# Third layer of a four-layer graph network: the accumulator banks are emptied by ScalarE copies and joined in SBUF; the fourth layer's score banks move

## Chip, cores and metric

One kernel runs on one core of a Trainium2 chip. The metric is device time in microseconds for one execution, the median of several runs. Matrix products, accumulated in PSUM, are TensorE's (PE in the profile). VectorE (DVE), ScalarE (ACT) and GpSimd (POOL) do the element-wise work, and SyncE (SP) issues most of the DMAs.

## The reference

Four layers of graph attention work one after another on the same 4096 nodes with 256 features, all with one 4096 x 4096 adjacency matrix, in float32. Each layer's result is added to its input and normalised. The change touches the third layer (`L2` in the reference) and the start of the fourth (`L3`):

```python
def _L2_gnn_ref(x, adj, W, a):
    h = x @ W
    e_src = h @ a[:D, 0]
    e_dst = h @ a[D:, 0]
    e = e_src[:, None] + e_dst[None, :]
    e = jnp.where(e > 0, e, NEG_SLOPE * e)
    att_logits = jnp.where(adj > 0, e, MASK_VAL)
    attention = jax.nn.softmax(att_logits, axis=1)
    h_prime = attention @ h
    return jax.nn.elu(h_prime)

def _L3_gnn_ref(features, adj, Wq, Wk):
    Qn = _cos_normalize(features @ Wq.T)
    Kn = _cos_normalize(features @ Wk.T)
    raw_att = Kn @ Qn.T
    att = jnp.where(adj > 0, raw_att, NEG) * TEMP
    att = jax.nn.softmax(att, axis=1)
    prop_fea = att @ features
    ...
    return (1.0 - KEEP_RATIO) * prop_fea + KEEP_RATIO * features

x = _layernorm(x + _L2_gnn_ref(x, adj, L2_gnn_W, L2_gnn_a), axis=-1)
x = _layernorm(x + _L3_gnn_ref(x, adj, L3_gnn_Wq, L3_gnn_Wk), axis=-1)
```

## The kernel before, in words

**Tiling.** The nodes are 32 tiles of 128. Output rows are taken in `NB` = 8 blocks of 512 (`QW`), and for every block the kernel walks over all 32 tiles of neighbours, two tiles at a time: `NP` = 16 units `g` for each block `b`.

**A unit of the third layer** (`additive_one`). The function `weights(b, g)` makes the unnormalised attention weights. For each of the two tiles ScalarE writes a factor `r` into one of two PSUM banks (L564), and VectorE turns it into `prob` with the mask (L565). From block 1 on, `mix_weights` forms four half-width sums and differences of `prob` for a seven-product scheme: one VectorE instruction (L434, both inputs in SBUF) and two GpSimd instructions (L435, L436). `sums(b, g)` then issues the matrix products (L444): seven products a unit from block 1 on, into four accumulator banks `acc0` to `acc3`; block 0 uses ordinary products (L579) into `acc0` and `acc1`. The first product of a unit writes `acc3`, the next two `acc0`, then two `acc1` and two `acc2`.

**Order.** The loop runs over units with a lag: iteration `i` makes the weights of unit `i` and the sums of unit `i - 3`. The order of TensorE, VectorE and ScalarE in this loop is the written one (`tc.manual_schedule`); GpSimd and the DMA queues are ordered by the framework's planner. The four accumulator banks have one copy, so the products of a new block write the banks that the block before has just filled, and these have to be read out in between. `prob` and `mix` have four buffers each.

**End of a block.** The iteration that sums unit 15 of block `b` comes to `weights(b + 1, 2)`. Before these weights are issued, `first_half` and `second_half` combine the four banks into the tile `quarters`: one ScalarE copy `one` (L449) and five VectorE additions that read one operand from PSUM (L450, L452, L453, L457, L458). In block 0 one ScalarE copy (L587) and two VectorE copies (L588, L589) do it.

**After a block.** While the next block runs, `finish` projects the four row tiles of the finished one (`project`, L594, products into the two `g` banks), takes them out of the bank (`take`: a VectorE reciprocal L600, ScalarE `e` L602 and `h` L603), adds and normalises them (L611, L612, L154, L155). From block 2 on, `follow.prepare` also prepares the fourth layer's inputs from the normalised rows: transposes by DMA (L127, L131, L135), products into both `g` banks (L1059, in the iteration of `g` = 8), squares, a root and scaling on ScalarE.

**Start of the fourth layer** (`cosine_attention`). Its code is outside the written order, so the planner places it. Scores (L1115) go to the two banks of the pool `co_pz`, and in later blocks also to `g`; ScalarE takes the exponential (L1119), VectorE masks (L1127) and mixes, and the same seven products follow. [...] The third layer's pools are opened in the order `gb_pr` (two factor banks), `gb_pa` (four accumulators), `gb_ps` (two `g` banks). The fourth layer's are opened as `co_pa`, `co_pz`, `co_ps`, so that its accumulators lie over the factor banks and `acc0`, `acc1`, and its score banks lie over `acc2`, `acc3` of the third layer.

Of the kernel before, what the change touches and what calls it, by code (L numbers as in the profile page):

```python
# [9 lines left out]
FP = mybir.dt.float32  # L10
# [4 lines left out]
OP = mybir.AluOpType  # L15
AX = mybir.AxisListType
PSUM = bass.MemoryType.PSUM

P = 128
# [3 lines left out]
QW = QB * P  # L23
# [5 lines left out]
def kernel(  # L29
# [27 lines left out]
    nc = tc.nc  # L57
    N = x.shape[0]
    NT = N // P
    NB = N // QW  # L60

    def pool(stack, name, bufs, **kw):
        return stack.enter_context(tc.tile_pool(name=name, bufs=bufs, reuse_waits="tile", **kw))
# [4 lines left out]
    fin1 = ctx.enter_context(tc.tile_pool(name="fin1", bufs=1))  # L68
# [352 lines left out]
    NP = NT // 2  # L421
    HW = QW // 2
# [9 lines left out]
    def mix_weights(s, z, eng):  # L432

        nc.vector.tensor_tensor(s[:, :2, :], z[:, 0, :].rearrange("p (h i) -> p h i", h=2), z[:, :, HW:], OP.subtract)  # L434
        eng.tensor_tensor(s[:, 2, :], z[:, 0, :HW], s[:, 1, :], OP.subtract)  # L435
        eng.tensor_tensor(s[:, 3, :], z[:, 1, :HW], s[:, 2, :], OP.subtract)  # L436

    def product(acc, z, s, t, g, n):

        even, odd = X[:, 2 * g, :D], X[:, 2 * g + 1, :D]  # L440
        at, half, w, a = ((3, 0, even[:, :P], z[:, 0, :HW]), (0, 0, odd[:, :P], z[:, 1, :HW]),
                          (0, 1, t[:, 1], s[:, 2]), (1, 0, t[:, 0], s[:, 1]), (1, 1, odd[:, P:], s[:, 3]),
                          (2, 0, t[:, 2], s[:, 0]), (2, 1, t[:, 3], z[:, 1, HW:]))[n]
        nc.tensor.matmul(acc[at][:, half * HW:(half + 1) * HW], w, a, start=(g == 0 and half == 0),  # L444
                         stop=(g == NP - 1), skip_group_check=True)

    def first_half(c, one, acc):

        nc.scalar.copy(one, acc[3][:, :HW])  # L449
        nc.vector.tensor_tensor(c[:, :2, :], one.unsqueeze(1).to_broadcast([P, 2, HW]),  # L450
                                acc[0].rearrange("p (h i) -> p h i", h=2), OP.add)
        nc.vector.tensor_tensor(c[:, 2, :], c[:, 1, :], acc[1][:, :HW], OP.add)  # L452
        nc.vector.tensor_tensor(c[:, 3, :], c[:, 2, :], acc[1][:, HW:], OP.add)  # L453

    def second_half(c, acc):

        nc.vector.tensor_tensor(c[:, 1:3, :], c[:, 1:3, :], acc[2][:, :HW].unsqueeze(1).to_broadcast([P, 2, HW]), OP.add)  # L457
        nc.vector.tensor_tensor(c[:, 1, :], c[:, 1, :], acc[2][:, HW:], OP.add)  # L458

    def quarters(c, k):  # L460

        lo = k % 2 * P
        return [c[:, q, lo:lo + P] for q in ((0, 3), (1, 2))[k // 2]]
# [61 lines left out]
    def additive_one(w_sb, ga, tail, op, follow):  # L525

        with ExitStack() as lay:
# [4 lines left out]
            sb = pool(lay, "gb_sb", 2)  # L532
# [9 lines left out]
            mixed, acc, prob, mix, mvs, roots, kept, drawn, ys, far_y = {}, {}, {}, {}, {}, {}, {}, {}, {}, {}  # L542

            def bank():
                return ps.tile([P, QW], FP, name="g")

            def weights(b, g):
                if b == 0 and g < 2:
                    mask = ga.first_mask[:, 2 * g:2 * g + 2, :]
                else:  # L550
                    mask = mp.tile([P, 2, QW], I32, name="mask")
                    nc.sync.dma_start(mask, edges[:, 2 * g:2 * g + 2, b * QW:(b + 1) * QW])
                if b < NB - 1:
                    if 4 <= g < 4 + QB:
                        ga.dots((b + 1) * QB + g - 4, (0,), sb, "h")
                    elif g == 8:
                        ga.sources(b + 1)
                    elif g == 11:
                        ga.row(b + 1, nc.sync)
                z = prob[b, g] = zp.tile([P, 2, QW], FP, name="prob")  # L560
                for n in range(2):
                    j = 2 * g + n
                    r = pr.tile([P, QW], FP, name="r")
                    nc.scalar.activation(r, ga.row_of(b), AF.Relu, bias=ga.less[:, j:j + 1], scale=ga.dst[:, j:j + 1])  # L564
                    nc.vector.scalar_tensor_tensor(z[:, n, :], r, ga.own[:, j:j + 1], mask[:, n, :], OP.add, OP.mult)  # L565
                if b:
                    s = mix[b, g] = zp.tile([P, 4, HW], FP, name="mix")
                    mix_weights(s, z, nc.gpsimd)

            def sums(b, g):  # L570
                if g == 0:
                    acc[b] = [pa.tile([P, QW], FP, name=f"acc{n}") for n in range(4)]
                if b:
                    for n in range(7):
                        product(acc[b], prob[b, g], mix[b, g], mixed[g // 2][:, g % 2], g, n)
                else:
                    for j in range(2 * g, 2 * g + 2):
                        for c in range(KC):
                            nc.tensor.matmul(acc[b][c], X[:, j, c * P:(c + 1) * P], prob[b, g][:, j % 2, :],  # L579
                                             start=(j == 0), stop=(j == NT - 1))  # L580
                if g == NP - 1:
                    c = kept[b] = op.tile([P, 4, HW], FP, name="quarters")
                    if b:
                        first_half(c, op.tile([P, HW], FP, name="one"), acc[b])
                        second_half(c, acc[b])
                    else:
                        nc.scalar.copy(c[:, :2, :], acc[b][0].rearrange("p (h i) -> p h i", h=2))  # L587
                        nc.vector.tensor_copy(c[:, 3, :], acc[b][1][:, :HW])  # L588
                        nc.vector.tensor_copy(c[:, 2, :], acc[b][1][:, HW:])  # L589

            def project(bank, b, k):
                po = drawn[b, k] = bank()
                for c, quarter in enumerate(quarters(kept[b], k)):
                    nc.tensor.matmul(po[:, :D + 1], quarter, w_sb[:, c, :D + 1], start=(c == 0), stop=(c == KC - 1))  # L594
# [52 lines left out]
            with tc.manual_schedule(engines=fixed):  # L647
                for i in range(len(units) + LAG):
                    b, g = units[i - LAG] if i >= LAG else (-1, 0)
                    if g == NP - 1:  # L650
                        sums(b, g)
                    if i < len(units):
                        weights(*units[i])
                    if b >= 0:
                        if g < NP - 1:
                            sums(b, g)
                        if b:
                            finish(b - 1, g)
                        else:
                            for _ in range(3 if g > 3 else 0):  # L660
                                next(before, None)
                            if g == 11:
                                follow.start()
                            elif g == 14:
                                follow.centre(bank())
                            if g % 2:
                                t = mixed[g // 2] = keep.tile([P, 2, 4, P], FP, name=f"mixed{g // 2}")
                                mix_features(t, g // 2)
                        if b > 1 and g in (2, 4, 6, 8, 9, 10, 11, 12, 13, 14, 15):
                            follow.prepare(bank, b - 2, 1, ys[b - 2])  # L670
                        if b == NB - 1 and g > 3 and g % 2 == 0:
                            q = g // 2 - 2
                            nc.scalar.dma_start(X[:, q * QB:(q + 1) * QB, :D], far_y[q])
                        if b == NB - 1 and g in (3, 5, 7):
                            follow.load_mask(0, (g - 3) // 2, prob[b, g][:, 0, :1])
# [411 lines left out]
    def cosine_attention(co, tail):  # L1087
# [4 lines left out]
        with ExitStack() as lay:  # L1092
            keep = pool(lay, "co_mixed", 1)
            sb = pool(lay, "co_sb", LAST + 1)
# [2 lines left out]
            co.turning = (pool(lay, "co_turn", 1), None,  # L1097
                          pool(lay, "co_turn_far", 2, space=bass.MemoryType.DRAM))

            pa = pool(lay, "co_pa", 1, space=PSUM)  # L1100
            pz = pool(lay, "co_pz", 2, space=PSUM)
            ps = pool(lay, "co_ps", 2, space=PSUM)
            ov = out.rearrange("(t p) d -> p t d", p=P)
            mixed, acc, prob, mix, y = {}, {}, {}, {}, {}
# [125 lines left out]
            for i in range(len(units) + LAG):  # L1230
                if i < len(units):
                    b, j = units[i]
# [5 lines left out]
                    if (b, j) in steps:  # L1238
                        n, step = steps[b, j]
                        co.prepare(bank, n, step, X[:, n * QB:(n + 1) * QB, :])  # L1240
                if i >= LAG:
                    b, j = units[i - LAG]
# [38 lines left out]
    with ExitStack() as weights1, ExitStack() as den1, ExitStack() as weights3:  # L1281
# [25 lines left out]
        op = weights3.enter_context(tc.tile_pool(name="gb_o", bufs=1))  # L1307
# [37 lines left out]
```

## Time and profile before

| what | value |
|---|---|
| median of 3 runs | 2818.91 us (2817.45 to 2821.47) |
| the profiled execution's own time | 2817.77 us |
| its span, first to last instruction | 2816.0 us |
| busy over the span: PE, DVE, ACT, POOL | 2784.7, 2274.4, 1695.6, 1050.6 us |
| third layer, blocks 1 to 7 (1772 to 2172 us): PE, DVE, ACT, POOL busy | 389.3, 329.9, 229.3, 197.7 of 400 us |
| passage to the fourth layer (2172 to 2186 us): PE, DVE, ACT, POOL busy | 10.9, 8.8, 5.0, 2.3 of 14 us |
| fourth layer (2186 to 2816 us): PE, DVE, ACT, POOL busy | 620.3, 429.8, 175.3, 46.6 of 630 us |
| mean granted TensorE clock over the span | 0.997 of full speed |

An engine is busy while it executes an instruction; register, branch, semaphore and DMA-issuing instructions are not counted. The profile pairs each idle stretch of an engine with the instruction or the DMA whose semaphore ended it. In a timeline a line has the start in microseconds from the first instruction, the duration of the merged group, the engine, the line of code, the operation, tiles written and read, the shape and the count. In brackets stands the idle time just before it and what ended it. One float32 product of this kernel shows as two matrix-product records and two weight loads.

### The profile page before, as it was taken

What the parts mean: (1) busy time and instruction counts of PE and PEld (TensorE: products, weight loads), DVE (VectorE), ACT (ScalarE), POOL (GpSimd) and SP (SyncE); (2) the same over time, 40 slices, a digit from 0 to 9 for tenths busy, and PEclk for the clock granted to TensorE, in tenths of its full rate; (3) what the DMA queues carried; (4) which work ended last, traced back from release to release, by engine and by line L of the source; (5) the groups of instructions that cost most, each with busy time, mean ns of one, the idle gap of its engine ahead of it and who ended that gap; (6) DMA issues with size and microseconds to landing.
All of it is one profiled execution on the core that took longest, in us unless ns stands there. A gap on an engine that the chain in (4) does not pass through costs nothing. (4 is left out here: it accounts for less than half of the span.)

```text
span 2816.0 us, 50179 instructions
## 1 busy us (share of the span) xinstructions
PE 2784.7 (99%) x19505; PEld 1434.6 (51%) x19505; DVE 2274.4 (81%) x3034; ACT 1695.6 (60%) x2641; POOL 1050.6 (37%) x983
## 2 busy tenths in 40 slices
PE   9999999999999999999999999999999999999998
PEld 5333333333443333333333334788887777777776
DVE  8899999999677788887887888888877766666665
ACT  8899999999246666666666665555565422222222
POOL 0001001001039878879778782454455100000000
PEclk9999999999999999999999999999999999999999
DMA  7566766665439899898998997576767544444441
GB/s 208 109 136 137 141 144 139 132 136 105 90 96 191 186 184 194 189 194 179 193 186 186 193 184 182 169 201 179 201 186 235 94 67 60 61 67 61 60 58 32
DMA packets 243650, 404.59 MB, mean 144 GB/s; under 512 B 25185, under 2 KB 126033, under 8 KB 242514
## 3 DMA queue, kind: packets, MB, share of 16 engines
q0 software_dynamic: 104176, 182.74, 41.0%
q1 hardware_dynamic: 132720, 211.41, 25.2%
q10 hardware_dynamic: 6514, 7.23, 0.7%
q8 instruction: 153, 2.51, 0.4%
q14 instruction: 87, 0.71, 0.1%
HBM read 332.27 MB, written 35.73 MB: 131 GB/s over the span
## 5 line engine op out<-in xcount | busy, mean ns | idle before, releaser
L830 DVE TENSOR_TENSOR prob<-p,mask 128x1024 f32<-128x1024 f32 x512 | 619.8, 1221 | 168.2 <-ACT p L820 162.1
L820 ACT ACTIVATE p<-p,shift 128x1024 f32<-128x1024 f32 x512 | 555.6, 1088 | 317.8 <-PE p L818 317.8
L310 PE MATMUL acc<-prob,V 128*32 128x512 f32 x6144 | 664.0, 592 | 1.2 <-DVE prob L300 1.2
L297 ACT ACTIVATE prob<-row,dst 128x512 f32<-128x512 f32 x1020 | 635.1, 712 | 0.6
L300 DVE SCALAR_TENSOR_TENSOR prob<-prob,mask 128x2048 f32<-128x2048 f32 x256 | 580.1, 2284 | 25.9 <-ACT prob L297 25.2
L840 POOL TENSOR_TENSOR den<-den,prob 128x1024 f32<-128x1024 f32 x220 | 558.1, 2537 | 95.8 <-DVE prob L830 84.9
L818 PE MATMUL p<-qT,kT 64*64 64x512 f32 x4096 | 531.1, 590 | 0.8 <-DVE prob L830 0.8
L854 PE MATMUL acc<-prob,V 64*64 64x512 f32 x4096 | 529.9, 589 | 0.0
L310 PEld LDWEIGHTS acc<-prob,V 128*32 128x32 f32 x6144 | 197.3, 110 | 453.0 <-issue 431.6
L444 PE MATMUL acc<-mix,mixed 128*128 128x256 f32 x1440 | 390.0, 380 | 1.7 <-DVE quarters L458 1.0
L854 PEld LDWEIGHTS acc<-prob,V 64*64 64x64 f32 x4096 | 157.4, 133 | 282.1 <-issue 280.3
L818 PEld LDWEIGHTS p<-qT,kT 64*64 64x64 f32 x4096 | 154.4, 133 | 277.4 <-issue 257.4
L444 PEld LDWEIGHTS acc<-mix,mixed 128*128 128x128 f32 x1440 | 272.2, 190 | 42.1 <-PE acc L444 2.9
L1127 DVE TENSOR_TENSOR prob<-prob,mask 128x1024 f32<-128x1024 f32 x128 | 156.4, 1222 | 168.9 <-ACT prob L1119 167.0
L90 POOL COPY tick<-prob 128x1 f32<-128x1 f32 x35 | 38.5, 1100 | 642.4 <-DVE prob L300 641.5
L444 PE MATMUL acc<-prob,X 128*128 128x256 f32 x960 | 250.5, 380 | 8.6 <-DVE quarters L450 8.6
L846 POOL DMA_DIRECT2D den<-prob x240 | 226.8, 945 | 59.0 <-DVE prob L830 26.0
L1046 POOL DMA_DIRECT2D mask<-in_adjT x64 | 47.7, 745 | 516.7 <-DVE prob L1127 430.3
L565 DVE SCALAR_TENSOR_TENSOR prob<-r,own,mask 128x512 f32<-128x512 f32 x252 | 177.1, 743 | 64.0 <-POOL mix L436 21.3
L444 PEld LDWEIGHTS acc<-prob,X 128*128 128x128 f32 x960 | 181.6, 190 | 92.2 <-issue 62.4
L1119 ACT ACTIVATE prob<-p 128x512 f32<-128x512 f32 x144 | 86.1, 598 | 222.1 <-PE p L1115 209.8
L1119 ACT ACTIVATE prob<-g 128x512 f32<-128x512 f32 x112 | 66.8, 596 | 194.0 <-PE g L1115 194.0
(220 smaller groups left out, 2810.3 us busy)
## 6 DMA issues: line engine op xcount, KB each, us to landing
mask<-in_adjT SPq DMA_DIRECT2D x254, 512.0 KB
den<-prob POOLq DMA_DIRECT2D x240, 512.0 KB, 5.2
mask<-edges SPq DMA_DIRECT2D x512, 64.0 KB
mask<-in_adjT POOLq DMA_DIRECT2D x64, 512.0 KB, 5.7
edges<-in_adj POOLq DMA_DIRECT2D x32, 512.0 KB, 10.0
far<-squares SPq DMA_DIRECT2D x16, 512.0 KB
den<-prob SPq DMA_DIRECT2D x16, 512.0 KB
row<-far SPq DMA_DIRECT2D x7, 1024.0 KB
```

The source lines that it names most:

```text
L297: nc.scalar.activation(z[:, h, :], r, AF.Relu, bias=-1.0, scale=dst[:, j, h:h + 1])
L300: nc.vector.scalar_tensor_tensor(z, z, 1.0, mask[m][:, j % MJ, :].unsqueeze(1).to_broadcast([P, H, QW]), OP.add, OP.mult)
L310: nc.tensor.matmul(acc[b][h * G:(h + 1) * G, n, :], part, prob[b, j][:, h, :], start=(j == 0), stop=(j == NT - 1))
L444: nc.tensor.matmul(acc[at][:, half * HW:(half + 1) * HW], w, a, start=(g == 0 and half == 0), stop=(g == NP - 1), skip_group_check=True)
L565: nc.vector.scalar_tensor_tensor(z[:, n, :], r, ga.own[:, j:j + 1], mask[:, n, :], OP.add, OP.mult)
L818: nc.tensor.matmul(p[c * d:(c + 1) * d, r, :], kT[half, c, at:at + d], qT[half, c, cols], start=True, stop=True)
L820: nc.scalar.activation(p, p, AF.Exp, bias=shift)
L830: nc.vector.tensor_tensor(z, p, mask[m][:, j % MJ, :].unsqueeze(1).to_broadcast([P, KC, QW]), OP.mult)
L840: nc.gpsimd.tensor_tensor(to, to, flat, OP.add)
L846: nc.gpsimd.dma_start(to, flat, accum_op=OP.add)
L854: nc.tensor.matmul(acc[b][c][r * d:(r + 1) * d, :], V[half, j, r * d:(r + 1) * d], prob[b, j][half, r, :], start=(j == 0), stop=(j == NH - 1))
L1127: nc.vector.tensor_tensor(z, z, co.mask[b, 2 * g // MJ][:, lo:lo + 2, :], OP.mult)
```

## The change

There are three edits.

1. Blocks 1 to 6 of the third layer: at the end of a block ScalarE copies all four banks as they are into SBUF (`one`, the two halves of `quarters`, and `two`, which uses the tile `kept0`). VectorE then adds in SBUF. Three of its five additions (`first_half_taken`) stand where `first_half` stood; the other two (`second_half_taken`) are issued after `weights(b + 1, 2)`. Block 7 keeps `first_half` and `second_half`.
2. Block 0: the two VectorE copies of `acc1` become ScalarE copies.
3. Fourth layer: `co_pz` is opened ahead of `co_pa`, so that the score banks lie over the two factor banks and the accumulators over the accumulators.

```diff
+    def taken(c, one, two, acc):
+
+        nc.scalar.copy(one, acc[3][:, :HW])
+        for n, sb in enumerate((c[:, :2, :], c[:, 2:, :], two)):
+            nc.scalar.copy(sb, acc[n].rearrange("p (h i) -> p h i", h=2))
+
+    def first_half_taken(c, one):
+        nc.vector.tensor_tensor(c[:, :2, :], one.unsqueeze(1).to_broadcast([P, 2, HW]), c[:, :2, :], OP.add)
+        for n in (2, 3):
+            nc.vector.tensor_tensor(c[:, n, :], c[:, n - 1, :], c[:, n, :], OP.add)
+
+    def second_half_taken(c, two):
+        nc.vector.tensor_tensor(c[:, 1:3, :], c[:, 1:3, :], two[:, 0, :].unsqueeze(1).to_broadcast([P, 2, HW]), OP.add)
+        nc.vector.tensor_tensor(c[:, 1, :], c[:, 1, :], two[:, 1, :], OP.add)
+
...
                 if g == NP - 1:
                     c = kept[b] = op.tile([P, 4, HW], FP, name="quarters")
-                    if b:
-                        first_half(c, op.tile([P, HW], FP, name="one"), acc[b])
+                    one = op.tile([P, HW], FP, name="one")
+                    if b == NB - 1:
+                        first_half(c, one, acc[b])
                         second_half(c, acc[b])
+                    elif b:
+                        two = fin1.tile([P, QW], FP, name="kept0").rearrange("p (h i) -> p h i", h=2)
+                        taken(c, one, two, acc[b])
+                        first_half_taken(c, one)
+                        return lambda: second_half_taken(c, two)
                     else:
                         nc.scalar.copy(c[:, :2, :], acc[b][0].rearrange("p (h i) -> p h i", h=2))
-                        nc.vector.tensor_copy(c[:, 3, :], acc[b][1][:, :HW])
-                        nc.vector.tensor_copy(c[:, 2, :], acc[b][1][:, HW:])
+                        nc.scalar.copy(c[:, 3, :], acc[b][1][:, :HW])
+                        nc.scalar.copy(c[:, 2, :], acc[b][1][:, HW:])
+                return lambda: None
...
                     b, g = units[i - LAG] if i >= LAG else (-1, 0)
-                    if g == NP - 1:
-                        sums(b, g)
+                    later = sums(b, g) if g == NP - 1 else lambda: None
                     if i < len(units):
                         weights(*units[i])
+                    later()
...
+            pz = pool(lay, "co_pz", 2, space=PSUM)
             pa = pool(lay, "co_pa", 1, space=PSUM)
-            pz = pool(lay, "co_pz", 2, space=PSUM)
             ps = pool(lay, "co_ps", 2, space=PSUM)
```

## The prediction

> **What bounds the kernel now.** I read the busy shares first, then TensorE's waits in the third layer, VectorE's waits there, one block boundary in the timeline, and the passage to the fourth layer.
>
> ```profile
> PE 2784.7 (99%) x19505; PEld 1434.6 (51%) x19505; DVE 2274.4 (81%) x3034; ACT 1695.6 (60%) x2641; POOL 1050.6 (37%) x983
> ```
>
> TensorE looks like the bound everywhere, but at 99% busy it can still be paced by others. Its waits from 1768 to 2200 us (total, times, longest):
>
> ```profile
> PE acc L444 <- DVE quarters L450: 8.6, 6, 1.8
> PE g L594 <- DVE quarters L453: 2.5, 1, 2.5
> ...
> PE g L1059 <- ACT h L603: 0.4, 2, 0.2
> ```
>
> The first line is what the change removes: six boundaries at which a new block waits for a bank that VectorE has not read out. In TensorE's timeline the first unit of a block starts its successor after 4.09, 5.53, 5.62, 5.62, 6.52 and 5.24 us; undisturbed units take 3.02. That is 14.5 us over the six. The next question is whether this time is lost or merely slack. VectorE's waits in the same stretch:
>
> ```profile
> DVE prob L565 <- POOL mix L436: 21.3, 13, 1.6
> ...
> DVE prob L565 <- ACT r L564: 11.5, 5, 2.3
> ...
> DVE quarters L450 <- PE acc L444: 0.9, 1, 0.9
> ...
> DVE rden L600 <- PE g L594: 0.7, 1, 0.7
> ```
>
> VectorE hardly ever waits for TensorE: once at L450 and once at L600, both after block 7, when the layer is over (and 0.9 us at L588, the end of block 0). ScalarE's r, e and h wait for VectorE, GpSimd's mix waits for VectorE's L434. So VectorE, ScalarE and GpSimd form a loop that runs free of TensorE. Its period is the distance of successive L450: 1882.7, 1941.0, 1999.3, 2057.4, 2116.2, so about 58.3 us. TensorE's own work in such a block is 16 x 3.02, four projections of 0.86 and 3.45 at L1059: 55.2 us. **The loop is the longer one, and the stall at the boundary is TensorE waiting for it.** The third line of TensorE's waits says where they meet again. The second half of L1059 needs the g bank that h (L603) of the last row tile frees; in the middle blocks TensorE waits there too, and in the others I find it 0.4 to 0.7 us behind h. Here is the boundary after block 3:
>
> ```profile
> 1940.40 0.69 DVE L434 TENSOR_TENSOR mix<-prob 128x512 f32<-128x512 f32 x1
> 1941.01 0.68 DVE L450 TENSOR_TENSOR quarters<-one,acc 128x512 f32<-128x512 f32 x1
> 1941.24 0.72 POOL L435 TENSOR_TENSOR mix<-prob,mix 128x256 f32<-128x256 f32 x1 [1.17 <-DVE mix L434]
> ...
> 1941.74 0.70 PE L444 MATMUL acc<-prob,X 128*128 128x256 f32 x2 [1.77 <-DVE quarters L450]
> ...
> 1943.49 0.42 DVE L458 TENSOR_TENSOR quarters<-quarters,acc 128x256 f32<-128x256 f32 x1
> 1943.83 1.40 DVE L565 SCALAR_TENSOR_TENSOR prob<-r,own,mask 128x512 f32<-128x512 f32 x2
> ...
> 1944.61 1.48 ACT L564 ACTIVATE r<-first_row,less,dst 128x512 f32<-128x512 f32 x2 [3.39 <-DVE prob L565]
> ```
>
> VectorE has no gap here. Its five additions take 2.82 us (1941.01 to 1943.83) while GpSimd mixes beside it. ScalarE idles 3.39 us. Now the passage to the fourth layer:
>
> ```profile
> 2174.92 0.71 DVE L127 STREAM_TRANSPOSE squares<-X 128x512 f32<-128x512 f32 x1 [2.53 <-DMA far<-squares]
> ...
> 2175.99 2.08 PE L594 MATMUL g<-w_sb,quarters 128*128 128x257 f32 x4 [2.47 <-DVE quarters L453]
> ...
> 2178.69 5.62 PE L1115 MATMUL p<-T 128*128 128x512 f32 x8 [0.62 <-PE g L594]
> ```
>
> L453 stands behind a transpose that waits for a DMA, TensorE idles 2.47 us, and its clock falls: the window 2178 to 2180 shows 0.50. The first score starts only at 2178.69, just after L458 (2178.19, 0.40 us) has read acc2. From 2172.27 to 2185.67 TensorE does 16 projection records of 0.215 and 8 score records of 0.43: 6.9 us of work in 13.4, so 6.5 us are lost.
>
> **What the Trainium skill says.** "SBUF — State Buffer", section "Who interferes with whom": a VectorE instruction with two SBUF inputs contends with a GpSimd instruction that reads SBUF, one with at most one SBUF input doesn't. The trace agrees in direction:
>
> ```profile
> 1957.66 0.84 POOL L435 TENSOR_TENSOR mix<-prob,mix 128x256 f32<-128x256 f32 x1 [2.48 <-DVE rden L600]
> 1957.95 0.83 DVE L612 TENSOR_TENSOR y<-X,e 128x256 f32<-128x256 f32 x1
> ...
> 2179.85 0.41 DVE L612 TENSOR_TENSOR X<-X,e 128x256 f32<-128x256 f32 x1
> ```
>
> The same addition takes 0.83 us beside L435 and 0.41 alone; L450 and L452, one input in PSUM, keep 0.68 and 0.42 beside it. The page says that the loser is blocked altogether; here it advances at some 45% of its speed (0.336 us of work in 0.75 us of overlap), and I use that. "TensorE: Matmul & The Clock Gate", "What's actually happening": the clock is halved after an idle window of about 3.4 us. Here a 2.5 us idle stretch was enough, and 6.8 us ran at half speed.
>
> **The change part by part.**
>
> *Banks emptied by ScalarE, blocks 1 to 6.* Added: three copies of 128x512 a boundary, at L587's 0.59 us: 1.77 us of ScalarE. After block 3 one ends at 1939.0, so acc0, acc1, acc2 are free by 1939.6, 1940.1, 1940.7. TensorE's products would reach them at 1939.6, 1940.5, 1941.3: the boundary stall goes. Queued behind the copies on ScalarE are the two r of the next unit. They start at 1940.7 instead of 1939.74; VectorE wants them at 1943.4 and nobody waits. Cost nothing, covered by the 3.39 us of ScalarE idle time; without that cover 1.77 us a block.
>
> *The five additions from SBUF.* The same count and sizes, so nothing is taken off VectorE; but L435 and L436 of the last unit run beside the first three. These have 1.53 us of work; with GpSimd reading from 0.23 to 2.0 us they end at 2.5. The last two come after L434 of the next unit, whose mix follows at once: 1.1 us of work become 2.1 if GpSimd mixes then, and stay 1.1 if it is still held by its T DMAs (L135), which from block 2 on come at this place (1945.11 to 1946.79). Against 2.82 us before, L565 of the unit after comes 0.7 us late in the second case and 1.6 in the first; of this 0.1 to 0.5 is given back, because L434 and L502 then meet GpSimd less. I take 1.5 after block 1, which has no T DMAs, and 0.8 after each of five others (0.6 to 1.1; below zero is excluded only if contention holds for these lines too, and I keep -0.15 each without it). Sum 5.5 us.
>
> *Block 0.* VectorE loses two copies, 0.84 us, but ScalarE has two more of 0.37 (L449's size) after 1772.26, so r starts about 0.9 later and L565 0.7 later (1773.65 for 1772.93). VectorE has no gap behind it: +0.7.
>
> All of it lies on the loop, and TensorE comes off its old wait at L450 only to wait for h at L1059, and here and there for L436. So the third layer ends 5.5 + 0.7 = **6.2 us later** (range -0.2 to 8.4).
>
> *Score banks over the factor banks.* These are last read by L565 of the last unit, at 2165.8, so the first scores need no L458. TensorE can fill 2172.4 to 2176 with up to four scores of 0.86 us, as ScalarE's exponentials (0.60) free the two banks; the clock then stays up. Of the 6.5 us lost I take 4.5 as saved: about 1 remains in waits for banks and for L453, and 1 goes to the first products of the fourth layer, whose prob and mix VectorE has to make while it is busy without a gap (2183 to 2199). Bounds: 1 us, if the planner leaves the projections ahead of the scores, to 6.5. It can't be much below zero, since no work is added. After this the fourth layer is TensorE's (no waits after 2195 but 1.3 us), so what is saved stays. No DMA is added or moved by the change itself; SP's queue is not passed by anything.
>
> Sum: +6.2 - 4.5 = **+1.7 us** against the profiled execution's own 2817.8 (span 2816.0 and 1.8 around it), so 2819.5; the median stands 1.1 us above this execution, so **2820.5 us**.
>
> **The rivals.**
>
> *The stalls were truly lost time.* Then all 14.5 us come back, and up to 6.5 at the passage: 2818.9 - 21 = 2798; half of it would be 2808. For it speaks that TensorE is busy 99% and that no other wait of it is large. Against it: the loop has no waits for TensorE and is 3 us longer, and the waits at L1059. It needs a loop that shortens.
>
> *The loop gets longer than is saved (slower).* GpSimd's mixes meet both groups of additions at each boundary: six times 1.6 and 0.7 are 10.3 us; with 2 us saved at the passage 2827. It decides once the boundaries cost over 1.6 each on average with less than 4.7 saved. For it: L612, always beside L435, takes the doubled 0.83 each time. Against: the T DMAs hold GpSimd in five of six blocks.
>
> *Nothing at the passage.* The planner keeps its order and TensorE still idles behind L453: 2818.9 + 6.2 - 1 = 2824; this lies inside the likeliest case's own range.
>
> **How the numbers follow.** A difference of 0.2%, 5.6 us, is about what a measurement of this kernel can tell from no change. Likeliest, 0.50: the loop sets the third layer, its growth and the gain at the passage nearly cancel; own range 2814 to 2826. Stalls truly lost, in whole or half: 0.22. Contention dominates: 0.28. Of the likeliest case a little reaches over each edge: faster 0.23, within 0.47, slower 0.30. The range 2802 to 2830 leaves out the lower part of the first rival and the extreme of the second.
>
> **What would show it.** In the profile after: no wait for L450 at the first six boundaries; the period of successive additions still 58 us or more; TensorE's waits for h at L1059 grown from 0.4 to some 10 us or more; the first additions from SBUF at about 1.2 us instead of 0.68; L1115 starting ahead of the last L453, with the clock at 1.00 through the passage. A period near 56 us would prove me wrong about the loop; a clock of 0.5 at the passage, about the gain there.

## The result, and the profile after

The changed kernel takes **2825.3 us** in the median of 15 runs, the kernel before 2819.7 in runs on the same chip. The ratio is **1.0021, 95% interval 1.0014 to 1.0027**: some 5.6 us slower, at the very edge of what the prediction said could be told from no change. The predicted time was 2820.5, the range 2802 to 2830, so the time lies inside it; but it isn't where the sum put it, and two of the terms were wrong. That range also holds the figures of the rivals (2808 for half of the stalls, 2824, 2827), so lying inside it doesn't tell the mechanisms apart. The profiled execution's span is 2823.5 us, 7.5 above that of before.

Some line numbers move: L564, L565 become L579, L580; L594 becomes L616; L600, L602, L603 become L622, L624, L625; L1059 becomes L1081; L1115, L1119, L1127 become L1137, L1141, L1149. New are the copies (L462 `one`, L464 the three banks), the first joins (L467, L469) and the second (L472, L473).

First the busy shares of the page, which hardly move:

```profile
PE 2784.3 (99%) x19505; PEld 1435.6 (51%) x19505; DVE 2279.4 (81%) x3032; ACT 1704.7 (60%) x2661; POOL 1054.0 (37%) x983
```

Then TensorE's waits from 1768 to 2225 us in the kernel after (what waited, for what: us in total, times, longest), which answer to those shown of before:

```profile
PE g L1081 <- ACT h L625: 11.0, 5, 3.0
PE g L1081 <- DMA xT<-far: 4.0, 1, 4.0
PE p L1137 <- ACT prob L1141: 2.4, 1, 2.4
PE acc L444 <- POOL mix L435: 1.8, 2, 1.1
```

The wait for L450 (8.6 us, six times) is gone, as the change meant. It is not won: TensorE now waits 11.0 us for `h`, the place where it met the loop before with 0.4. The time has moved within the block, it has not left it. The third line is new and will explain the passage.

VectorE's waits in the third layer of the kernel after:

```profile
DVE prob L580 <- POOL mix L436: 21.3, 13, 1.6
DVE prob L580 <- ACT r L579: 16.0, 7, 2.3
...
DVE prob L580 <- DMA mask<-in_adjT: 4.2, 1, 4.2
...
DVE prob L580 <- PE acc L444: 2.3, 1, 2.3
DVE quarters L450 <- PE acc L444: 1.9, 1, 1.9
```

The last line is the wait after block 7. The 2.3 us at L580 for TensorE stand at the start of block 3, where blocks 4 to 7 wait the same 2.3 us for ScalarE's `r`; a wait for several semaphores is put down to the one that came last. So the loop of VectorE, ScalarE and GpSimd runs as free of TensorE as it did. New in size is the wait for a mask transfer, in block 7, which will explain part of the loss. Before it was

```profile
DVE prob L565 <- DMA mask<-in_adjT: 2.0, 1, 2.0
```

The boundary after block 3, timeline of the kernel after (start, duration, engine, line, operation):

```profile
1942.79 1.08 ACT L464 COPY quarters<-acc 128x512 f32<-128x512 f32 x2
...
1943.73 0.62 ACT L464 COPY kept<-acc 128x512 f32<-128x512 f32 x1
...
1944.90 0.69 DVE L467 TENSOR_TENSOR quarters<-one,quarters 128x512 f32<-128x512 f32 x1
...
1945.13 1.03 POOL L435 TENSOR_TENSOR mix<-prob,mix 128x256 f32<-128x256 f32 x1 [1.17 <-DVE mix L434]
...
1945.69 1.62 DVE L469 TENSOR_TENSOR quarters<-quarters 128x256 f32<-128x256 f32 x2
...
1947.23 1.40 DVE L580 SCALAR_TENSOR_TENSOR prob<-r,own,mask 128x512 f32<-128x512 f32 x2
```

The copies empty the banks while TensorE is still busy with the next products, and the two engines then take turns. VectorE's L467 started first and keeps its 0.69 us; GpSimd's L435, which starts in its middle, takes 1.03 instead of 0.73 and ends 0.57 us after L467 is over at 1945.59, so most of its work comes after that moment. Then L469 pays: its two additions take 1.62 us together where they had 0.42 each. The first group ends 2.4 us after it began.

The passage to the fourth layer, timeline after:

```profile
2181.26 1.88 PE L1137 MATMUL p<-T 128*128 128x512 f32 x4
...
2183.36 0.38 DVE L453 TENSOR_TENSOR quarters<-quarters,acc 128x256 f32<-128x256 f32 x1
```

The scores go ahead of L453, without a wait, and the clock there is 1.00. So the bank swap does what it says. Yet the fourth layer begins no earlier relative to the third. From the end of the last L565 (L580) to the first L450 of the fourth layer's blocks the traces show 100.53 us before and 100.24 after. Here is where the gain went, some 30 us later, in the timeline of the kernel after:

```profile
2205.94 1.22 DVE L1149 TENSOR_TENSOR prob<-prob,mask 128x1024 f32<-128x1024 f32 x1
...
2206.60 2.90 POOL L166 TENSOR_TENSOR s<-r 128x8 f32<-128x8 f32 x1 [6.08 <-ACT r L160]
...
2209.02 0.42 DVE L436 TENSOR_TENSOR mix<-prob,mix 128x256 f32<-128x256 f32 x1
...
2210.39 2.17 ACT L1097 ACTIVATE rows<-g,r 128x128 f32<-128x128 f32 x8 [3.87 <-POOL r L169]
...
2212.40 1.13 ACT L1141 ACTIVATE prob<-p 128x512 f32<-128x512 f32 x2
...
2213.10 1.22 PE L1137 MATMUL p<-T,T 128*128 128x512 f32 x1 [2.36 <-ACT prob L1141]
```

Read it upwards. TensorE waits 2.36 us for an exponential. The exponential stands on ScalarE behind the row scaling L1097, and that waited 3.87 us for a root that GpSimd computes from 128x8 values. The first of GpSimd's four instructions (L166) took 2.90 us. In the timeline of the kernel before it took 0.24:

```profile
2197.68 0.24 POOL L166 TENSOR_TENSOR s<-r 128x8 f32<-128x8 f32 x1 [10.17 <-ACT r L160]
```

In the kernel after it ends at 2209.50, just after VectorE's unbroken chain of seven instructions with two SBUF inputs, from L1149 to L436, ends at 2209.44. After this wait TensorE runs 3.4 us at half clock, as the table of stretches shows (length; busy us and instructions of PE, PEld, DVE, ACT, POOL; clock; DMA):

```profile
2213.10:2216.50 3.40, 3.40 (x6) 2.10 (x7) 3.40 (x7) 1.03 (x2) 0.80 (x1) 0.50 0.38 154
```

The wait and the half clock (3.4 us of time for 1.7 of work) are 4.1 us, about the gain that had been predicted.

### The profile page after: what moved, and what is told of

Same layout as the page of the kernel before. It is cut to its first block, busy times and chain, and to the rows that moved or that the text cites. A ratio compares the mean times of both kernels' runs of the same rounds, so it can differ in the third digit from the quotient of the medians.

```text
span 2823.5 us, 50201 instructions
## 1 busy us (share of the span) xinstructions
PE 2784.3 (99%) x19505; PEld 1435.6 (51%) x19505; DVE 2279.4 (81%) x3032; ACT 1704.7 (60%) x2661; POOL 1054.0 (37%) x983
## 5 line engine op out<-in xcount | busy, mean ns | idle before, releaser
L1149 DVE TENSOR_TENSOR prob<-prob,mask 128x1024 f32<-128x1024 f32 x128 | 156.5, 1223 | 165.4 <-ACT prob L1141 165.1
L580 DVE SCALAR_TENSOR_TENSOR prob<-r,own,mask 128x512 f32<-128x512 f32 x252 | 177.1, 743 | 67.3 <-POOL mix L436 21.3
L1141 ACT ACTIVATE prob<-p 128x512 f32<-128x512 f32 x144 | 85.8, 598 | 221.0 <-PE p L1137 208.5
L1141 ACT ACTIVATE prob<-g 128x512 f32<-128x512 f32 x112 | 66.8, 596 | 194.0 <-PE g L1137 194.0
```

## The experiments

All kernels were timed with the kernel before on the same chip, in three groups of four (`e1` to `e4`, `e5` to `e8`, `e9` to `e12`); the four of a group share the runs of the kernel before.

**Each half of the change alone.** `e1_banks` is the kernel before with nothing but the pools swapped:

```diff
+            pz = pool(lay, "co_pz", 2, space=PSUM)
             pa = pool(lay, "co_pa", 1, space=PSUM)
-            pz = pool(lay, "co_pz", 2, space=PSUM)
```

> The kernel before with the third edit alone (score banks over the factor banks); the bank read-out is the old one. The loop theory (VectorE, ScalarE and GpSimd set the third layer's pace, TensorE waits for them): the third layer stays as before, the scores fill the passage, so faster than before by 1 to 4.5 us; in the profile the first score starts ahead of L453 and the clock is at full speed there. The stall theory (TensorE's stalls at the block boundaries are lost time) says the same for this edit, since it leaves the boundaries alone. If the passage is paced by VectorE's work after it, no gain: within 0.7 us.

Measured: 2820.5 us, ratio 1.0002 (0.9994 to 1.0010): nothing. Its trace gives 99.50 us for the distance from the last L565 to the first L450, 1.0 less than before (how far this distance varies is said further down), and TensorE's waits say why it isn't more:

```profile
PE acc L444 <- DVE quarters L450: 8.9, 6, 1.8
PE p L1115 <- ACT prob L1119: 2.4, 1, 2.4
```

The wait behind L453 is gone and the wait for the exponential has come, with half clock behind it.

`e2_copies` is the changed kernel with the pools back in the old order, that is, the third layer's two edits alone:

```diff
+            pa = pool(lay, "co_pa", 1, space=PSUM)
             pz = pool(lay, "co_pz", 2, space=PSUM)
-            pa = pool(lay, "co_pa", 1, space=PSUM)
```

> The first two edits alone (ScalarE empties the banks, joins in SBUF); score banks as before. Loop theory: the loop grows by 0.6 to 1.5 us at each of six boundaries and 0.7 at block 0, so 5 to 9 us slower than before. Stall theory: the 14.5 us of stalls come back, 2805 us or less against 2819.

Measured: 2823.8 us, ratio 1.0015 (1.0008 to 1.0021), so 2.3 to 5.9 us slower. The whole of the change's loss is in these two edits, within the intervals. Of TensorE's waits the loop's mark is the same as after:

```profile
PE g L1081 <- ACT h L625: 10.8, 5, 2.5
```

**Is the boundary's stall lost time or slack?** Two kernels push the loop from both sides. `e3_nojoin` takes the five additions of blocks 1 to 6 out of the changed kernel:

```diff
+                    if 0 < b < NB - 1:
+                        c = kept[b] = kept[0]
...
-                        taken(c, one, two, acc[b])
-                        first_half_taken(c, one)
-                        return lambda: second_half_taken(c, two)
+                        c = fin1.tile([P, QW], FP, name="kept1"), fin1.tile([P, QW], FP, name="kept2")
+                        nc.scalar.copy(one, acc[b][3][:, :HW])
+                        nc.scalar.copy(c[0], acc[b][0])
+                        nc.scalar.copy(c[1], acc[b][1])
+                        nc.scalar.copy(two, acc[b][2].rearrange("p (h i) -> p h i", h=2))
```

> The changed kernel without the five additions in blocks 1 to 6: ScalarE still copies all four banks into SBUF, but nothing joins them, and the projections of these blocks read block 0's tile (leaves out the joining of the third layer's sums in six blocks). VectorE loses about 4 us a block against the changed kernel, 2.8 against the one before; TensorE's work and its freedom at the boundary are those of the changed kernel. Loop theory: the period falls from 58 to about TensorE's own 55.2 us, so some 10 to 18 us below the kernel before. Stall theory: as the changed kernel, about 5 us above the kernel before, since TensorE's stalls are gone in both.

Measured: 2809.2 us, ratio 0.9965 (0.9952 to 0.9978). With the copies in place and the stall gone in both, taking work off VectorE gains 16 us against the changed kernel. The mark in the profile came only in part. The period, from a block's first L580 to the next one's, is 55.6 us in block 2, but 57.8 on average in blocks 3 to 6, for 58.9 in the kernel after. Of the 11.1 us by which the third layer is shorter than in that trace, 4.5 are block 7's, where the kernel after waits for a mask transfer. And the projections read an old tile here, so they wait for no join.

`e4_extra` is the kernel before with one more row sum on VectorE in unit 6 of blocks 1 to 7, far from any boundary:

```diff
+                    if g == 6:
+                        nc.vector.tensor_reduce(fin.tile([P, 2], FP, name="extra"), z, AX.X, OP.add)
```

> The kernel before with one more VectorE instruction of about 1.2 us (a row sum over prob, used by nobody) in unit 6 of blocks 1 to 7, far from the boundaries. TensorE has 4 to 6 us of slack there. Loop theory: every one lengthens the loop, 7 x 1.2 us less 0.7 of slack: 6.5 to 8.5 us slower. Stall theory: nothing, within 1 us.

Measured: 2827.7 us, ratio 1.0032 (1.0020 to 1.0045). The row sum takes 1.21 us in the trace, and seven of them are 8.5. TensorE's waits:

```profile
PE acc L444 <- DVE quarters L450: 9.1, 6, 1.8
PE g L1061 <- ACT h L605: 7.9, 6, 2.1
```

Were the stall at L450 the bound, TensorE would have absorbed this. Instead nearly all of it reaches the end, at the place where the loop and TensorE meet (L1061 here). **The stall theory falls.**

**ScalarE's copies and VectorE's additions apart.** `e7_copies_only` is the kernel before with three more copies of the banks on ScalarE, read by nobody:

```diff
                         second_half(c, acc[b])
+                        if b < NB - 1:
+                            for n in range(3):
+                                nc.scalar.copy(fin1.tile([P, QW], FP, name=f"kept{n}"), acc[b][n])
```

> The kernel before, its five additions read PSUM as they do there; ScalarE in addition copies the three banks of sums (128x512 each) into spare tiles at each of the boundaries of blocks 1 to 6, and nothing reads the copies. It splits the cost of edit 1 into ScalarE's part and VectorE's part. My prediction's step (three copies are covered by 3.39 us of ScalarE idle time): within 1 us of before. If ScalarE's copies delay r: six times 0.6 to 1.8, so 4 to 11 us slower. A further 0 to 1 us may come from banks held a little longer.

Measured: 2824.9 us, ratio 1.0018 (1.0011 to 1.0026). This looked like a refutation of "the copies cost nothing", but ScalarE's waits show another thing:

```profile
ACT kept L588 <- DVE quarters L450: 15.6, 6, 2.7
...
ACT kept L588 <- DVE quarters L458: 4.3, 6, 0.7
```

Here two engines read the same banks and the copies stand in line behind VectorE's additions, and the next `r` behind the copies: VectorE's waits for `r` grow from 11.5 to 20.2 us. In the change nothing stands before the copies. The run isn't a clean test, so `e12_act_time` copies a tile of SBUF instead:

```diff
+                                nc.scalar.copy(fin1.tile([P, QW], FP, name=f"kept{n}"), prob[b, g][:, n % 2, :])
```

> The kernel before, ScalarE in addition copying a 128x512 tile of edge weights in SBUF three times at each of the boundaries of blocks 1 to 6 into spare tiles that nothing reads: ScalarE's time of edit 1 without the banks, and without the waits for VectorE that the copies of banks had. My prediction's step (covered by 3.39 us of ScalarE idle time): within 1 us of before. If ScalarE's queue is part of what sets the loop there: six times 0.5 to 1.8, so 3 to 11 us slower, 2823 to 2831.

Measured: 2821.4 us, ratio 1.0001 (0.9992 to 1.0009). ScalarE's time is covered, as predicted; what `e2_copies` loses is not ScalarE's time as such.

`e6_second` puts the last two additions of each boundary on GpSimd in the changed kernel:

```diff
     def second_half_taken(c, two):
-        nc.vector.tensor_tensor(c[:, 1:3, :], ...
-        nc.vector.tensor_tensor(c[:, 1, :], ...
+        nc.gpsimd.tensor_tensor(c[:, 1:3, :], ...
+        nc.gpsimd.tensor_tensor(c[:, 1, :], ...
```

> The changed kernel with the last two additions of each boundary in blocks 1 to 6 (L472, L473) on GpSimd instead of VectorE. VectorE's loop loses 1.1 to 1.6 us a boundary. If VectorE alone sets the loop: six times 1.1 to 1.6, so 7 to 10 us below the changed kernel, 2815 to 2818. If the loop runs through GpSimd as well (VectorE's wait for the mix of L436 is 21.3 us over the layer) or the two engines' lock hands the time back: within 3 us of the changed kernel or above it, 2822 to 2832. If the stall at the banks were the bound: no difference.

Measured: 2824.9 us, ratio 1.0017 (1.0010 to 1.0024), no different from the changed kernel. On GpSimd the two take 1.28 and 0.90 us, and TensorE's first wait is now for it:

```profile
PE acc L444 <- POOL mix L435: 8.4, 6, 1.8
```

I read this as GpSimd being no freer than VectorE just behind the boundary; that was not tested apart.

**The passage: was the gain earned and given back?** `e5_root` adds to `e1_banks` that the four small root instructions run on VectorE in the last block:

```diff
-            end_root(v, r, QB * 2, nc.gpsimd)
+            end_root(v, r, QB * 2, nc.vector if b == NB - 1 else nc.gpsimd)
```

> The kernel before with the two pools swapped (edit 3, which alone measured 1.0002) and, in addition, the four small instructions of the inverse root of the last block (L1072 into L166 to L169, 128x8) on VectorE instead of GpSimd. In the bank swap's trace the first of these took 2.90 us on GpSimd instead of 0.24, ending just as VectorE's chain of SBUF instructions ended; ScalarE's row scaling (L1075) waited 3.87 us for them, the exponential stood behind it, TensorE idled 2.36 us and then ran 3.4 us at half clock: about 4 us. Theory (the passage's gain was earned and given back through GpSimd being held off by VectorE): the wait of TensorE for the exponential goes, and the time falls by 3 to 4.5 us against before, 2815.5 to 2818. Rival (the passage is paced by VectorE's work after it): within 1 us of before, with another wait in its place.

Measured: 2818.7 us, ratio 0.9997 (0.9989 to 1.0005). The edit missed its aim: the root at the passage is that of block 6, and GpSimd's line is still there, in the timeline of `e5_root`:

```profile
2202.66 2.90 POOL L166 TENSOR_TENSOR s<-r 128x8 f32<-128x8 f32 x1 [6.08 <-ACT r L160]
```

`e9_root2` takes blocks 6 and 7 (`b >= NB - 2`).

> The kernel before with the two pools swapped, and the four small instructions of the inverse root on VectorE for the last two blocks (6 and 7); the passage's one is block 6, which the run before this one had missed. Theory (the passage's gain is earned and then given back, because GpSimd's first small instruction is held off by VectorE for 2.90 us, ScalarE's row scaling waits 3.87 us and the exponential behind it comes late): TensorE's wait of 2.4 us for the exponential goes, with it the half clock behind it where it occurred, and the time falls 2 to 4.5 us below before: 2815.5 to 2818. Rival (what is saved is lost to whatever comes next): within 1 us of before, ratio 0.9997 to 1.0003.

Measured: 2816.0 us, ratio **0.9983 (0.9975 to 0.9990)**, 4.8 us below before. TensorE's waits up to 2225 us hold neither L453 nor the exponential:

```profile
PE acc L444 <- DVE quarters L450: 8.4, 6, 1.8
PE g L1059 <- ACT h L603: 3.2, 3, 1.2
```

On VectorE the first of the four takes 0.16 us (at 2203.98 in its timeline). The distance from the last L565 to the first L450 falls to 94.34 us, 6.2 less than before and 5.2 less than with the swap alone. So the two edits together earn time where the swap alone earns none, and the wait that goes is the one behind the held-off root. The root on VectorE without the swap was not run, so the swap's own share isn't shown. Part may be the planner's: with this edit it also puts one exponential ahead of the row scaling.

**Shorten the loop.** `e8_gp_add` is the kernel before with the residual addition L612 on GpSimd, and the row statistics behind it one unit later:

```diff
-                nc.vector.tensor_tensor(ys[b][:, k, :], x, e, OP.add)
-                one_row(mvs[b], k, ys[b][:, k, :])
+                if b < NB - 1:
+                    nc.gpsimd.tensor_tensor(ys[b][:, k, :], x, e, OP.add)
...
+                if g in (5, 6, 8, 10):
+                    k = (5, 6, 8, 10).index(g)
+                    one_row(mvs[b], k, ys[b][:, k, :])
```

> The kernel before with the residual addition of the third layer (L612, X + e, 128x256, four in each of blocks 0 to 6) on GpSimd instead of VectorE, and its row statistics one unit later. VectorE loses four times 0.41 (alone) to 0.83 us (beside L435), 1.7 to 3.3 us a block; GpSimd gains four times 0.73. If VectorE's own work sets the loop: six or seven blocks by 1.7 to 3 us, down to where TensorE's own 55.2 us a block takes over, so 8 to 18 us faster, 2802 to 2812. If GpSimd is as much a part of the loop, or the lock between the two hands it back: within 4 us of before or slower.

Measured: 2813.5 us, ratio 0.9977 (0.9969 to 0.9985). The loop shortens from 58.4 to 56.9 us in blocks 3 to 6, less than hoped, and VectorE's first wait is now another:

```profile
DVE prob L565 <- ACT r L564: 46.3, 28, 2.3
```

ScalarE's `r` takes over where GpSimd's mix was, and the waits for mask transfers grow from 2.0 to 14.6 us. `e11_after_gp` does the same to the changed kernel (same diff).

> The changed kernel with the residual addition of the third layer on GpSimd and its statistics one unit later. In that move's own trace VectorE waits 46 us for ScalarE's r and the period is 56.8 us; TensorE still waits 4.4 us for L450 and 1.2 us for L458 at the boundaries, against its own 55.2 us of work a block. Loop theory: the loop still sets the layer, now at ScalarE, so three more copies at each of six boundaries cost up to 6 x 1.8 us and the five contended additions add to it: 4 to 12 us above that move alone, 2817 to 2825. Stall theory (with the shorter loop the stall is lost time and the copies pay): 3 to 6 us below it, 2807 to 2811.

Measured: 2814.9 us, ratio 0.9980 (0.9973 to 0.9987). Neither expectation holds: it is neither 4 us above `e8_gp_add` nor 3 below. Blocks 0 to 6 take 391.8 us in its trace and 391.1 in that of `e8_gp_add`: there the copies neither pay nor cost, with the loop near TensorE's own time. Block 7 takes 59.8 us for 54.3, and VectorE waits 7.7 us for a mask transfer in it for 4.2; the executions of `e11_after_gp` spread from 2809.8 to 2819.9 us. How these parts add up was not taken apart.

`e10_best` joins what had gained: `e8_gp_add`, the swapped pools, and the roots of blocks 6 and 7 on VectorE.

> The kernel before with three edits: the residual addition L612 of the third layer on GpSimd with its statistics one unit later (alone 0.9977), the two pools swapped, the inverse roots of blocks 6 and 7 on VectorE. If the gains add: 6.4 us from the first and 2 to 4 from the passage, 2809 to 2812. If the passage gives it all back again: 2813 to 2815.

Measured: **2806.9 us, ratio 0.9952 (0.9938 to 0.9966)**, faster than both kernels. The two gains alone, 0.23% and 0.17%, make 0.40%, and the interval holds that. It leaves the copies out.

## Why the prediction was right or wrong, step by step

**The loop sets the third layer: right.** `e4_extra` and `e8_gp_add` move the time by lengthening and shortening VectorE's work with the wait for L450 in place, and the change removes that wait without gaining. TensorE's wait at L1081 was put at some 10 us or more and is 11.0.

**ScalarE's copies cost nothing: right** for ScalarE's time (`e12_act_time`). The cover holds only if nothing stands before the copies; in `e7_copies_only` they waited for VectorE, and that kernel is 0.18% slower.

**The five additions: right in sign, over-sized, and the mechanism misread.** I read from an addition of 0.83 us that the loser of the two engines goes on at 45% of its speed. The boundary shows turns instead: who starts first keeps its full speed, the other waits until it is over. That is what the Trainium skill's "SBUF — State Buffer", section "Who interferes with whom", says of the lock (whoever issues first has it for the whole instruction; "the other **fully blocks** (not throttle)"; the sentence is about other modes of VectorE, but the trace shows the same for two SBUF inputs), and the page was right where I put my reading in its place. So the mark I named, 1.2 us for the first addition, is wrong: L467 keeps 0.68 at all six boundaries, and L469 doubles to a median of 0.80 from 0.42. The group's length was nearly what I used, 2.4 for 2.5. The last two additions met GpSimd too: L473 takes 0.42 to 1.17 us, 0.97 in the median, for 0.42 before. I had counted on the T transfers to hold GpSimd in five of six blocks; after block 3 its L435 starts at 1950.12, between two of them at 1949.55 and 1950.78.

Two readings in the prediction are a little off, and nothing hangs on them. The groups of 2.5 and 1.1 or 2.1 us are 0.8 or 1.8 longer than 2.82, not 0.7 or 1.6; and the 6.52 us among the stalls contain part of a stretch at half clock that begins at 2059.73.

The sum along the loop was 6.2 us. The table has the period from a block's first L565 (L580) to the next one's, the third layer unchanged in four traces (before, `e1_banks`, `e5_root`, `e9_root2`: mean) and changed in two. The end of a block falls into the period of the next:

| period of block | unchanged | after | `e2_copies` | predicted growth |
|---|---|---|---|---|
| 0 | 51.59 | 51.48 | 51.68 | none |
| 1 | 56.34 | 56.72 | 56.72 | 0.7 |
| 2 | 56.94 | 58.11 | 58.08 | 1.5 |
| 3 to 6 | 234.84 | 235.62 | 236.13 | 0.8 each |
| 7 | 55.06 | 57.60 | 56.47 | 0.8 |
| growth in all | | 4.8 | 4.3 | 6.2 |

The end of block 0 costs 0.4 for 0.7, that of block 1 1.2 for 1.5. After blocks 2 to 5 it is 0.2 to 0.3 each, not 0.8, though every boundary has the same doubled additions; but the four unchanged traces differ by 2.5 us in these blocks, and `e12_act_time`, timed like the kernel before, has 237.0 there, so the number is soft. Whether the growth comes from reading SBUF or from moving two additions behind the next weights was not separated, and edit 2 was not run alone.

The last period grows by 1.4 to 2.5. In the kernel after most of that is a transfer, and here the step "SP's queue is not passed by anything" failed. VectorE waits for the mask of unit 11 in block 7 for 4.2 us, in the four unchanged traces for 1.8 to 2.4. This mask's transfer is issued right behind the four loads of turned rows (L135) on the same queue. The first of these loads is issued 10.1 us after the store that it reads (L131), at 2145.26 for 2135.19, and TensorE waits 4.0 us for them as well (L1081 above). In the kernel before it is 7.1 us, and 6.7 to 7.5 in all nine kernels without edit 1. With edit 1 it is 8.6 in `e2_copies` and 10.2 in `e11_after_gp`, but 7.3 in `e3_nojoin` and 6.6 in `e6_second`. So the change seems to have a part in it; why the store lands later was not settled.

Clear of the differences between executions are the ends of blocks 0 and 1 and the last period. The timed loss of `e2_copies`, 2.3 to 5.9 us, agrees with the table.

**The passage: the failed step.** The step was that "the fourth layer is TensorE's" and "what is saved stays", with 4.5 us saved. The first half came true: scores ahead of L453, the clock at 1.00, no idle time. What failed is "stays". TensorE came earlier to a place where ScalarE's queue hung on a GpSimd root that VectorE held off for 2.90 us, waited 2.36 us and lost another 1.7 at half clock. Net, in the time of `e1_banks`, nothing (-1.7 to +2.8 us), and `e9_root2` shows that with the root moved as well some 5 us were there to be had.

This doesn't hang on one trace. In all six kernels with the pools swapped and that root on GpSimd, its first instruction takes 2.90 us, and TensorE waits 2.4 to 2.8 us for the exponential. In the six with the old order of the pools it takes 0.23 to 0.26. The distance from the last L565 to the first L450 is 97.7 to 100.5 us with the old order and 97.0 to 101.2 with the swap, and 94.3 and 94.2 in `e9_root2` and `e10_best`.

The size of the gain was read from an unlucky execution. Around the passage the kernel before runs 6.8 us at half clock; of the five other kernels with the old order three run 3.4 us and two none. And the mark that I had named for the gain, scores ahead of L453 at a clock of 1.00, came true without it, because it stood 30 us too early.

That it "can't be much below zero" held. The lower bound of 1 us was in the prediction for another reason, that the planner might keep the projections ahead of the scores; it didn't keep them there.

**The rivals.** "Stalls truly lost" (2798 or 2808) falls with `e4_extra`. "Contention dominates" (2827) is near in time, but by the wrong road: it wanted 10.3 us at the boundaries and 2 saved, and there were 4 to 5 and none. "Nothing at the passage" (2824) is nearest, though its reason was the order. The measured loss is at 0.2%, where I had given most of the chance to the side within it.

## What to carry to other kernels

A wait on the busiest engine is lost time only if that engine sets the pace. Look at the period of the others, then lengthen their work on purpose: if the end moves by as much, the wait is slack, and removing it only moves it. Before counting a gain at a passage, follow every queue for the next tens of microseconds to the first wait that doesn't depend on it, and look there for what comes late. Where the clock takes part, read the size of a gain from more than one execution.

## What the runs showed of the hardware that I had not expected

A single small GpSimd instruction was held off until a chain of VectorE instructions without a gap had ended: 128x8 values took 2.90 us instead of 0.24, past the ends of six VectorE instructions, until the seventh was over. Six traces show it, each time with the end 0.06 us after the seventh's. At the boundaries, in contrast, GpSimd's L435 got its turn after one instruction; there L469 starts 0.10 us after L467's end, while in the chain each instruction starts before the one ahead has ended. That the gap decides is a reading of these two places and wasn't tested.

The Trainium skill's "TensorE: Matmul & The Clock Gate", section "What's actually happening", puts the halving after an idle window of about 3.4 us. In the kernel after 2.36 us of idle time were followed by 3.4 us at half clock, and in `e5_root` the same 2.36 us were not: its two scores took 1.12 us together at 2209.15, near the usual 1.02. Shorter waits did it too: in the kernel before the 1.77 us after block 5 were followed by 3.4 us at half clock (from 2059.73), the 1.77 us after block 3 were not. So less idle time than the page gives was enough here, and not every time; what decides isn't shown. A gain of a few microseconds can hang on it.
